# Two-layer transformer with experts: one gather of every four moved behind the scores, scalings spread over four waves, and a branch inside layer 1's run of waves

## The chip, the core and the metric

The kernel runs on one NeuronCore of one Trainium2 chip. The metric is the device time in microseconds of one execution. Three timed runs of the kernel before gave 1534.94, 1539.51 and 1540.47 us; the median is 1539.51 us. A separate execution was profiled.

## What is computed

Input is `x`, 8 sequences of 512 tokens with 256 features. Two layers follow each other, each an attention and a mixture of experts, each followed by a layer norm of (input + result). Cut to what matters here:

```python
x = layernorm(x + attn0(x))      # 16 heads of 16, causal towards later tokens (j >= i), softmax
x = layernorm(x + moe0(x))       # 7 experts 256->1024->256 with at most 512 tokens each, and a no-op expert; top 2
x = layernorm(x + attn1(x))      # rms norm, rotary, sigmoid scores divided by their sum
x = layernorm(x + moe1(x))       # 8 experts 256->512->256 and 4 that pass the token on; top 2
```

In `moe0` an expert takes the first 512 tokens, in order of the sequences, that chose it. If the first five sequences already fill every expert, the other three need not be dispatched. The kernel computes a flag `late` for the opposite case.

## The kernel before

**Waves.** Layer 0's attention runs as 8 x 16 waves (`waves0`, L1362). Wave `g` belongs to sequence `b = g // 16`, place `w = g % 16` in it. Four waves in a row are one group of four heads: `w // 8` is the half `m` of the features, `w // 4 % 2` the parity `t`. Within the group the four waves take the key blocks `jb` = 3, 2, 1, 0, with widths of 512, 384, 256 and 128 queries.

In each wave TensorE's order is written by hand (`tc.manual_schedule`), and each engine runs its own instructions in the order of the code:

1. `scores` (L583 on): four matmuls of the wave's width into two two-bank PSUM tiles `sc` (L588), an exponential for each on ScalarE (L597), a causal mask for each on GpSimd (L600, `affine_select`).
2. `lowered`, in waves with `w % 4 == 2`: four transposes (L580) into the bank `mm`, added to the queries by VectorE (L581).
3. the first steps of the plan.
4. `greatest` for the wave six ahead: four matmuls (L561) into two `sc` tiles, four reductions on VectorE (L569). Widths in the four waves of a group: 128, 256, 384, 512.
5. `gathered` for the wave before (kept in `waiting`): the exponentials times the values (L612), accumulated over the group in the bank `av`, widths 128, 512, 384, 256 in the four waves; after the last block ScalarE copies it out (L620).
6. the second steps of the plan.

PSUM has three `sc` tiles of two banks, one `av` and one `mm` bank in layer 0. The three `sc` tiles are taken in turn by scores and maxima, so that each use waits for the reader of the use three before. Every projection or transpose outside of 1, 4 and 5 goes through the one `mm` bank: the next such step waits until ScalarE or VectorE has emptied it.

**The plan.** `beside0` (L1290 on) lists for each place `w` the steps for other sequences: for the next one (`n`) its transposes (`turned_in`), queries and keys (`query`, one part of 256 tokens: 4 matmuls at L538, two evacuations on ScalarE at L545) and values (`value`, L521, copies at L525 and L530); for the last one (`a`) the way from attention to routing (`by_token`, `by_feature`, `projected`, `rooted`, `normed`, `logits`, `chosen`, `raised`); for the one before that (`z`) the rest of the routing and, from `w = 8`, the scatter of its rows to `xbuf` (L832, GpSimd's indirect DMA). `kept(b, c)` (L708) is the scaling of 128 tokens of the layer norm, in place, on ScalarE: 128x256 elements, four for each sequence.

**After seven sequences** come the seven experts of layer 0 (`experts0`), with a list of steps for sequences 5 and 6, one of which is taken at each of 50 gaps; then the eighth sequence's waves, with layer 1's first sequence prepared beside them; then layer 1's waves (`waves1`), in which `sc`, `av` and `mm` have two tiles each, and the gather of a wave stands behind the scores of the next.

**The branch.** After layer 1's first sequence, all engines load `late` into a register (L1656) and branch (L1657): if it is set, `again0` dispatches the last three sequences and runs the experts of layer 0 again. In this case's data it isn't set, and no instruction of `again0` appears in the trace. Ahead of it the last wave's gather is issued and the PSUM pools are closed; they are opened again behind it.

Of the kernel before, what the change touches and what calls it, by code (L numbers as in the profile page):

```python
# [43 lines left out]
def tile_two_layers(  # L44
# [41 lines left out]
    def psum(stack, sc, av, mm):  # L86

        for name, bufs in (("sc", sc), ("av", av), ("mm", mm)):
            p[name] = stack.enter_context(
                tc.tile_pool(name=f"p_{name}{sc}", bufs=bufs, space=PSUM)  # L90
            )
# [4 lines left out]
    def bank():  # L96
        return p["mm"].tile([P, 512], FP, tag="mm", name="mm")
# [1192 lines left out]
    def beside0(b, w):  # L1290

        z, a, n = b - 2, b - 1, b + 1
        t = l0
        plan = {
            -6: ([(t.value, n, 3)], []),
            -5: ([(t.value, n, 2)], []),
            -4: ([(t.value, n, 1)], [(t.query, n, 1, "q", 0)]),
            -3: ([(t.value, n, 0)], [(t.query, n, 1, "q", 1)]),  # L1300
            -2: ([], [(t.query, n, 1, "k", 0)]),
            -1: ([], [(t.query, n, 1, "k", 1)]),
            0: ([], [(t.turned_in, n, 0), (t.kept, z, 2), (t.kept, z, 3), (t.shared, z)]),
            1: ([(t.by_token, a, 0)], [(t.turned_in, n, 1), (t.pointed, z)]),
            2: ([], [(t.query, n, 0, "q", 0), (t.residual, n)]),
            3: ([(t.query, n, 0, "q", 1)], [(t.query, n, 0, "k", 0)]),
            4: ([(t.by_token, a, 1)], [(t.by_token, a, 2), (t.counted, z)]),
            5: ([(t.by_token, a, 3)], [(t.ranked, z)]),
            6: ([], [(t.query, n, 0, "k", 1), (t.sent, z)]),
            7: ([(t.by_feature, a, 0)], [(t.by_feature, a, 1)]),  # L1310
            8: ([(t.projected, a, 0)], [(t.projected, a, 1)]),
            9: ([(t.projected, a, 2)], [(t.projected, a, 3)]),
            10: ([], [(t.query, n, 1, "q", 0)]),
            11: ([(t.query, n, 1, "q", 1)], [(t.query, n, 1, "k", 0)]),
            12: ([(t.value, n, 3)], [(t.rooted, a)]),
            13: ([(t.value, n, 2)], [(t.normed, a), (t.logits, a)]),
            14: ([], [(t.query, n, 1, "k", 1), (t.chosen, a)]),
            15: (
                [(t.value, n, 1)],
                [(t.value, n, 0), (t.raised, a), (t.kept, a, 0), (t.kept, a, 1)],  # L1320
            ),
        }
        if b == B - 2:


            for i, lists in plan.items():
                plan[i] = tuple([s for s in steps if s[0] is not t.query] for steps in lists)
            plan[8] = ([(t.projected, a, 0)], [(t.query, n, 0, which, 0) for which in "qk"])
            plan[9] = ([(t.projected, a, 1)], [(t.query, n, 0, which, 1) for which in "qk"])
            plan[10] = ([], [(t.projected, a, 2)])  # L1330
            plan[11] = ([(t.projected, a, 3)], [])
        elif b == B - 1:

            u = l1
            plan = {
                0: ([], []),
                1: ([], []),
                2: ([], [(u.gather, 0, 0)]),
                3: ([], [(u.gather, 0, 1)]),
                4: ([], [(u.gather, 0, 2), (u.summed, 0, 0)]),  # L1340
                5: ([], [(u.gather, 0, 3), (u.summed, 0, 1)]),
                6: ([], [(u.summed, 0, 2)]),
                7: ([], [(u.summed, 0, 3)]),
                8: ([], [(u.normed, 0), (u.gather, 1, 0)]),
                9: ([], [(u.turned_in, 0, 0), (u.residual, 0), (u.gather, 1, 1)]),
                10: ([], [(u.turned_in, 0, 1), (u.gather, 1, 2)]),
                11: ([], [(u.query, 0, 0, "q", 0), (u.gather, 1, 3)]),
                12: ([], [(u.query, 0, 0, "q", 1)]),
                13: ([], [(u.query, 0, 0, "k", 0)]),
                14: ([], [(u.query, 0, 0, "k", 1)]),  # L1350
                15: ([], [(u.value, 0, 0), (u.value, 0, 1)]),
            }
        first, second = plan[w]
        if w >= 8 and z < EARLY:
            cs = [w - 8] if b < B - 2 else [2 * (w - 8), 2 * (w - 8) + 1]
            first = [(t.scatter, z, (c // 2, c % 2)) for c in cs if c < 2 * NC] + first
        return [[s for s in steps if 0 <= s[1] < B] for steps in (first, second)]
# [4 lines left out]
    def waves0(start, stop):  # L1362
        nonlocal waiting
        t = l0
        for g in range(start, stop):
            b, w = g // 16, g % 16
            now = None
            if g >= 0:
                now = t.scores(b, w // 8, w // 4 % 2, NC - 1 - w % 4)
                if w % 4 == 0:  # L1370
                    t.fill(b, w // 4)
                if w == 10 and b + 2 < B:
                    t.load_x(b + 2)
            if (g + 2) % 4 == 0 and 0 <= g + 2 < 16 * B:
                ob, ow = (g + 2) // 16, (g + 2) % 16
                t.lowered(ob, ow // 8, ow // 4 % 2)
            first, second = beside0(b, w if g >= 0 else g)
            if b == 0 and w in (1, 3, 4, 5, 8, 9, 12):
                fn, arg = t.rsteps.pop(0)
                fn(arg)  # L1380
                if w == 1:
                    t.residual(0)
            if b == 2 and w < len(l1.steps):
                fn, arg = l1.steps[w]
                fn(arg)
            run(first)
            ob, ow = (g + AHEAD) // 16, (g + AHEAD) % 16
            if ob < B:
                t.greatest(ob, ow // 8, ow // 4 % 2, (1, 0, 3, 2)[ow % 4])
            if waiting:  # L1390
                t.gathered(*waiting)
            run(second)
            waiting = now
# [76 lines left out]
                xes[e + 2] = tokens0(e + 2)  # L1470
        run(steps)

    def again0():


        with ExitStack() as ph:
            psum(ph, 1, 2, 2)
            rp = ph.enter_context(tc.tile_pool(name="redo", bufs=1))
            for b in range(EARLY, B):
                for c in range(NC):  # L1480
# [2 lines left out]
            for e in range(E0):  # L1483
# [6 lines left out]
                nc.sync.dma_start(out=xe, in_=xbuf[rows, :].rearrange("(c p) d -> p c d", p=P))  # L1490
                xeT = rp.tile([P, KC, S], FP, tag="xeT", name="xeT")
                for kc in range(KC):
                    ps = bank()
                    for c in range(NC):
                        nc.tensor.transpose(
                            ps[:, c * P : (c + 1) * P], xe[:, c, kc * P : (kc + 1) * P], ident
                        )
                    nc.vector.tensor_copy(xeT[:, kc, :], ps)
                for c in range(NC):
                    h = rp.tile([P, I0 // P, P], FP, tag="h", name="h")  # L1500
                    ps = wide().rearrange("p u (f t) -> p (u f) t", t=P)
                    for f in range(I0 // P):
                        for kc in range(KC):
                            nc.tensor.matmul(
                                out=ps[:, f, :], lhsT=wi[:, kc, f * P : (f + 1) * P],
                                rhs=xeT[:, kc, c * P : (c + 1) * P],
                                start=(kc == 0), stop=(kc == KC - 1),
                            )
                    nc.vector.tensor_scalar(h, ps, 0.0, None, ALU.max)
                    ps = bank()[:, :D]  # L1510
                    for f in range(I0 // P):
                        nc.tensor.matmul(
                            out=ps, lhsT=h[:, f, :], rhs=wo[:, f, :],
                            start=(f == 0), stop=(f == I0 // P - 1),
                        )
                    nc.vector.tensor_copy(xe[:, c, :], ps)
# [84 lines left out]
    with tc.manual_schedule():  # L1601
# [23 lines left out]
        steps = [(t.by_token, a, 0), (t.query, n, 1, "q", 0), (t.by_token, a, 1), (t.query, n, 1, "q", 1)]  # L1625
        steps += [(t.by_token, a, 2), (t.query, n, 1, "k", 0), (t.by_token, a, 3), (t.query, n, 1, "k", 1)]
        steps += [(t.by_feature, a, kc) for kc in range(KC)]
        steps += [(t.kept, z, c) for c in (2, 3)]
        steps += [(t.projected, a, c) for c in range(NC)]
        steps += [(fn, z) for fn in (t.shared, t.pointed, t.counted)]  # L1630
        steps += [(t.filled,)]
# [9 lines left out]
    rows1 = ExitStack()  # L1641
    l1p = rows1.enter_context(tc.tile_pool(name="l1p", bufs=1, side="right"))
    over = planp.tile([P, 1], I32, name="over")
    with tc.manual_schedule():
        waves0(16 * (B - 1), 16 * B)
        l0.gathered(*waiting)
        waiting = None
    banks.close()
    psum(banks, 2, 2, 2)
    with tc.manual_schedule():  # L1650
        waves1(0)
        l1.gathered(*waiting)
        waiting = None
    banks.close()
    alone.close()
    again = nc.values_load(late[0:1, 0:1], min_val=0, max_val=1)  # L1656
    with tc.If(again > 0):  # L1657
        again0()
    banks = ExitStack()
    psum(banks, 2, 2, 2)  # L1660
    ahead = ExitStack()
    lotp = ahead.enter_context(tc.tile_pool(name="lotp", bufs=1))

# [410 lines left out]
```

## Time and profile before

| What | Value |
|---|---|
| timed runs, median | 1539.51 us (1534.94 to 1540.47) |
| profiled execution | 1549.87 us |
| its span, first to last instruction | 1548.0 us |
| mean granted TensorE clock in it | 0.968 |
| first scores of sequences 1, 3, 4, 5 to those of the next (timeline) | 68.1, 70.1, 71.0, 71.7 us |
| layer 0's waves, sequences 0 to 6 / experts, first matmul to last / eighth sequence's waves | to 534 us / to 745 us / to 813 us |
| the branch on TensorE | 883 to 887 us |
| VectorE busy per 50 us in layer 0 (350 to 400 us) | 34.71 us |
| ScalarE, GpSimd, same stretch | 26.15, 18.89 us |

How to read it: a busy time is that of one engine, in the profiled execution. A group line gives the source line, the engine, the operation, what it writes and reads, how often, its busy time, the mean of one in ns, and the engine's idle time just before, with what ended most of it. A timeline line gives the start and the length in us, engine, line, operation, and in brackets the idle time before it and the engine, tile and line that ended that. PE is TensorE's matmuls, PEld its weight loads, PEq its instruction queue; ACT is ScalarE, DVE VectorE, POOL GpSimd. A line of windows gives a stretch, its length, the busy time of PE, PEld, DVE, ACT and POOL with their counts, the granted clock, the DMA share and GB/s. Four fp32 matmuls appear as eight instructions.

### The profile page before, as it was taken

What the parts mean: (1) busy time and instruction counts of PE and PEld (TensorE: products, weight loads), DVE (VectorE), ACT (ScalarE), POOL (GpSimd) and SP (SyncE); (2) the same over time, 40 slices, a digit from 0 to 9 for tenths busy, and PEclk for the clock granted to TensorE, in tenths of its full rate; (3) what the DMA queues carried; (4) which work ended last, traced back from release to release, by engine and by line L of the source; (5) the groups of instructions that cost most, each with busy time, mean ns of one, the idle gap of its engine ahead of it and who ended that gap; (6) DMA issues with size and microseconds to landing.
All of it is one profiled execution on the core that took longest, in us unless ns stands there. A gap on an engine that the chain in (4) does not pass through costs nothing. (4 is left out here: it accounts for less than half of the span.)

```text
span 1548.0 us, 24814 instructions
## 1 busy us (share of the span) xinstructions
PE 1414.4 (91%) x8574; PEld 759.5 (49%) x8574; DVE 877.7 (57%) x3287; ACT 689.6 (45%) x1079; POOL 480.7 (31%) x602
## 2 busy tenths in 40 slices
PE   7999889989998899999889899999999999999992
PEld 4444444444443466766434333333333344878881
DVE  4656666666766513121456466776766755553494
ACT  4455545454554321111335555666665666122242
POOL 2321233323233200000351224543643431342462
PEclk9999999999999999999989989999999999999996
DMA  8859950000000022231100000202302005557764
GB/s 245 250 164 361 356 187 13 19 7 25 2 22 4 29 82 82 82 120 57 42 28 8 22 8 30 38 27 23 46 22 28 19 16 158 182 179 241 271 221 158
DMA packets 136010, 149.86 MB, mean 97 GB/s; under 512 B 29645, under 2 KB 118890, under 8 KB 135874
## 3 DMA queue, kind: packets, MB, share of 16 engines
q1 hardware_dynamic: 118274, 121.51, 24.9%
q0 software_dynamic: 10560, 23.51, 6.2%
q10 hardware_dynamic: 7040, 3.15, 0.8%
q8 instruction: 72, 1.18, 0.3%
q14 instruction: 64, 0.52, 0.1%
HBM read 76.88 MB, written 77.10 MB: 99 GB/s over the span
## 5 line engine op out<-in xcount | busy, mean ns | idle before, releaser
L569 DVE CUSTOM_DVE_ANT_0 seen<-sc,shade 128x128 f32<-128x128 f32 (+3 forms) x512 | 251.1, 490 | 138.5 <-PE sc L561 109.8
L1035 ACT ACTIVATE e<-sc 128x1024 f32<-128x1024 f32 x256 | 248.5, 1021 | 150.3 <-PE sc L1027 139.9
L600 POOL TENSOR_SCALAR_AFFINE_SELECT e<-e 128x256 f32<-128x256 f32 x256 | 104.9, 416 | 590.0 <-ACT e L597 585.6
L597 ACT ACTIVATE e<-sc 128x1024 f32<-128x1024 f32 (+3 forms) x256 | 167.0, 702 | 125.9 <-PE sc L588 117.2
L1044 PE MATMUL av<-e,v 128*32 128x512 f32 x1024 | 140.7, 621 | 0.0
L561 PE MATMUL sc<-k,q 32*128 32x384 f32 (+3 forms) x1024 | 127.2, 499 | 12.7 <-DVE mpad L569 6.5
L588 PE MATMUL sc<-q,k 32*128 32x512 f32 (+3 forms) x1024 | 122.0, 491 | 3.6 <-DVE mpad L569 2.5
L612 PE MATMUL av<-e,v 128*32 128x512 f32 (+3 forms) x1024 | 99.4, 456 | 2.7 <-POOL e L600 2.3
L1753 PE MATMUL yp<-w_e,h 128*128 128x256 f32 x416 | 96.2, 384 | 3.0 <-DVE h L1745 3.0
L1457 PE MATMUL sc<-wo,h 128*128 128x256 f32 x448 | 98.7, 379 | 0.0
L1440 PE MATMUL sc<-xeT,wi 128*128 128x512 f32 x224 | 97.9, 592 | 0.0
L1737 PE MATMUL sc<-xtT,w_e 128*128 128x256 f32 x416 | 94.8, 380 | 0.2
L1457 PEld LDWEIGHTS sc<-wo,h 128*128 128x128 f32 x448 | 84.7, 190 | 11.7 <-issue 0.5
L1027 PE MATMUL sc<-q,k 16*128 16x512 f32 x512 | 82.6, 660 | 5.7 <-PEq L1657 2.2
L1027 PE MATMUL sc<-q,kb 32*128 32x512 f32 x512 | 81.4, 641 | 6.5 <-ACT e L1035 6.5
L1753 PEld LDWEIGHTS yp<-w_e,h 128*128 128x128 f32 x416 | 79.7, 193 | 14.9 <-DVE h L1745 3.8
L1764 POOL DMA_INDIRECT ybuf<-yt,to x52 | 51.0, 981 | 113.6 <-DVE yt L1763 101.8
L1737 PEld LDWEIGHTS sc<-xtT,w_e 128*128 128x128 f32 x416 | 77.1, 190 | 10.6 <-issue 1.2
L561 PEld LDWEIGHTS sc<-k,q 32*128 32x128 f32 x1024 | 52.7, 189 | 56.3 <-issue 25.4
L588 PEld LDWEIGHTS sc<-q,k 32*128 32x128 f32 x1024 | 49.3, 186 | 54.5 <-issue 33.6
L1210 POOL DMA_INDIRECT xbuf<-x,idx x64 | 68.4, 1068 | 23.7 <-issue 15.0
L898 POOL DMA_INDIRECT got<-ybuf,idx_all x64 | 65.7, 1027 | 17.3 <-issue 14.4
(304 smaller groups left out, 2094.5 us busy)
## 6 DMA issues: line engine op xcount, KB each, us to landing
xbuf<-blank SPq DMA_DIRECT2D x130, 272.0 KB
w_e<-in_w SPq DMA_DIRECT2D x104, 256.0 KB
ybuf<-blank SPq DMA_DIRECT2D x16, 512.0 KB
y<-ybuf SPq DMA_DIRECT2D x16, 512.0 KB
wi<-in_we_in SPq DMA_DIRECT2D x7, 1024.0 KB
wo<-in_we_out SPq DMA_DIRECT2D x7, 1024.0 KB
xt<-xbuf SPq DMA_DIRECT2D x26, 272.0 KB
own<-in_x SPq DMA_DIRECT2D x8, 512.0 KB
```

Source lines behind the costliest of these rows:

```text
L561: nc.tensor.matmul(out=places[r], lhsT=q["q", m, t][32 * r : 32 * r + 32, ib * P : (ib + 1) * P], rhs=q["k", m, t][32 * r : 32 * r + 32, i ...
L569: nc.vector.tensor_tensor_reduce(out=seen[:, :width], in0=places[r], in1=shade[:, :width], scale=-1.0, scalar=-MASKED, op0=ALU.add, op1=AL ...
L588: nc.tensor.matmul(out=places[r], lhsT=q["k", m, t][32 * r : 32 * r + 32, jb * P : (jb + 1) * P], rhs=q["q", m, t][32 * r : 32 * r + 32, : ...
L597: nc.scalar.activation(e[:, :, :width], s[:, :, :width], AF.Exp, scale=SCALE)
L600: nc.gpsimd.affine_select(out=own, in_=own, pattern=[[0, 2], [-1, P]], compare_op=ALU.is_ge, fill=0.0, base=0, channel_multiplier=1,)
L612: nc.tensor.matmul(out=q["av"][32 * r : 32 * r + 32, : (jb + 1) * P], lhsT=vs[b % 2][:, jb, 8 * m + 2 * r + t, :], rhs=es[r], start=(jb == ...
L1027: nc.tensor.matmul(out=scs[r // 2][:, r % 2, :], lhsT=k[32 * r : 32 * r + lanes, jb * P : (jb + 1) * P], rhs=q["q", m][32 * r : 32 * r + l ...
L1035: nc.scalar.activation(e, scs[pr], AF.Sigmoid, scale=SCALE)
L1044: nc.tensor.matmul(out=q["av"][32 * r : 32 * r + 32, :], lhsT=vs[b % 2][:, jb, 8 * m + 2 * r + t, :], rhs=es[r // 2][:, r % 2, :], start=( ...
L1457: nc.tensor.matmul(out=ps[:, c, :], lhsT=h[f][:, c * P : (c + 1) * P], rhs=wo[:, f, :], start=(f == 0), stop=(f == I0 // P - 1),)
L1737: nc.tensor.matmul(out=ps[:, f // 2, f % 2 * TB : (f % 2 + 1) * TB], lhsT=q.wi[kc][:, f * P : (f + 1) * P], rhs=q.xtT[:, kc, :], start=(kc ...
L1753: nc.tensor.matmul(out=q.ps[c], lhsT=q.h[:, f // 2, at : at + P], rhs=q.wo[f // 2][:, f % 2 * D : (f % 2 + 1) * D], start=(f == 0), stop=( ...
```

## The change

It has three parts. Nothing that is computed changes.

1. In `waves0`, in waves with `g % 4 == 3`, the gather of the wave before stands right behind the scores, ahead of the first steps and `greatest`. In the other waves it stays behind `greatest`.
2. In the plan, the four scalings `kept` of a sequence leave wave 15 (two of them) and wave 0 of the next sequence (two) for waves 2, 3, 6 and 7, one in each; they are last of their wave's second steps. One query part (key, part 1, `m` = 1) moves from wave 14 to wave 13, ahead of `normed` and `logits`. In the experts' step list, sequence 5 gets four scalings instead of two, since its wave 15 has none any more.
3. At the branch, the register load of `late` moves ahead of the eighth sequence's waves. The last gather of layer 1's first sequence isn't issued ahead of the branch but stays in `waiting`, so that it comes behind the first scores of the next sequence. The PSUM pools stay open; one `sc` and one `mm` tile are taken ahead of the branch for `again0`, which uses these two for everything.

The diff, cut to its core:

```diff
-            0: ([], [(t.turned_in, n, 0), (t.kept, z, 2), (t.kept, z, 3), (t.shared, z)]),
+            0: ([], [(t.turned_in, n, 0), (t.shared, z)]),
...
-            2: ([], [(t.query, n, 0, "q", 0), (t.residual, n)]),
-            3: ([(t.query, n, 0, "q", 1)], [(t.query, n, 0, "k", 0)]),
+            2: ([], [(t.query, n, 0, "q", 0), (t.residual, n), (t.kept, z, 0)]),
+            3: ([(t.query, n, 0, "q", 1)], [(t.query, n, 0, "k", 0), (t.kept, z, 1)]),
...
-            6: ([], [(t.query, n, 0, "k", 1), (t.sent, z)]),
-            7: ([(t.by_feature, a, 0)], [(t.by_feature, a, 1)]),
+            6: ([], [(t.query, n, 0, "k", 1), (t.sent, z), (t.kept, z, 2)]),
+            7: ([(t.by_feature, a, 0)], [(t.by_feature, a, 1), (t.kept, z, 3)]),
...
-            13: ([(t.value, n, 2)], [(t.normed, a), (t.logits, a)]),
-            14: ([], [(t.query, n, 1, "k", 1), (t.chosen, a)]),
-            15: (
-                [(t.value, n, 1)],
-                [(t.value, n, 0), (t.raised, a), (t.kept, a, 0), (t.kept, a, 1)],
-            ),
+            13: ([(t.value, n, 2)], [(t.query, n, 1, "k", 1), (t.normed, a), (t.logits, a)]),
+            14: ([], [(t.chosen, a)]),
+            15: ([(t.value, n, 1)], [(t.value, n, 0), (t.raised, a)]),
...
+            if g % 4 == 3 and waiting:
+                t.gathered(*waiting)
+                waiting = None
             if (g + 2) % 4 == 0 and 0 <= g + 2 < 16 * B:
...
-        steps += [(t.kept, z, c) for c in (2, 3)]
+        steps += [(t.kept, z, c) for c in range(NC)]
...
+    again = nc.values_load(late[0:1, 0:1], min_val=0, max_val=1)
     with tc.manual_schedule():
         waves0(16 * (B - 1), 16 * B)
...
     with tc.manual_schedule():
         waves1(0)
-        l1.gathered(*waiting)
-        waiting = None
-    banks.close()
     alone.close()
-    again = nc.values_load(late[0:1, 0:1], min_val=0, max_val=1)
+    places = wide(), bank()
     with tc.If(again > 0):
-        again0()
-    banks = ExitStack()
-    psum(banks, 2, 2, 2)
+        again0(*places)
```

Inside `again0`, `bank()` becomes the one `mm` tile and `wide()` the one `sc` tile, and its own pools go.

More of the change, by code (lines that the diff above doesn't have):

```diff
@@ L1471, in experts0, with again0 @@
         run(steps)
-    def again0():
+    def again0(inner, turned):
         with ExitStack() as ph:
-            psum(ph, 1, 2, 2)
             rp = ph.enter_context(tc.tile_pool(name="redo", bufs=1))
@@ L1492, in again0 @@
                 for kc in range(KC):
-                    ps = bank()
+                    ps = turned
                     for c in range(NC):
@@ L1500, in again0 @@
                     h = rp.tile([P, I0 // P, P], FP, tag="h", name="h")
-                    ps = wide().rearrange("p u (f t) -> p (u f) t", t=P)
+                    ps = inner.rearrange("p u (f t) -> p (u f) t", t=P)
                     for f in range(I0 // P):
@@ L1509, in again0 @@
                     nc.vector.tensor_scalar(h, ps, 0.0, None, ALU.max)
-                    ps = bank()[:, :D]
+                    ps = turned[:, :D]
                     for f in range(I0 // P):
```

## The prediction

> **What bounds the kernel now.** I read the page's busy table and slices first, then the groups of instructions by line, then the timeline over one sequence of layer 0 and over the branch. All sums below are made inside the profiled execution (span 1548.0 us, 1549.87 us with what lies around it). The median of the three timed runs is 1539.51 us, 0.7% less; I carry differences over to it unscaled.
>
> ```profile
> PE 1414.4 (91%) x8574; PEld 759.5 (49%) x8574; DVE 877.7 (57%) x3287; ACT 689.6 (45%) x1079; POOL 480.7 (31%) x602
> L561 PE MATMUL sc<-k,q 32*128 32x384 f32 (+3 forms) x1024 | 127.2, 499 | 12.7 <-DVE mpad L569 6.5 <-ACT e L597 5.5 <-ACT ye L1464 0.4
> L708 ACT ACTIVATE own<-own,less,r 128x256 f32<-128x256 f32 x32 | 17.5, 596 | 0.0
> ```
>
> TensorE is the bound, but not everywhere full. In layer 0 (to 534 us) it is some 90% busy. Adding up the bracketed idle times of the timeline by wave, sequences 3 to 5 lose 5.9 to 6.2 us each, of 70 to 72 us: 0.68 in each of waves 3, 7, 11 and 15, 0.91 in wave 14, 0.98 in wave 0, 0.29 in wave 1, 0.64 in wave 6, 0.33 in wave 9. In the expert stage it is 99% busy (49.65 of 50 us from 550 to 600), so nothing is won there.
>
> In a wave, S is the scores (L588), G the maxima's scores (L561, read by VectorE on L569), AV the gathered values (L612); the number is the width. The wave changed is S128, first steps, G512, AV256, second steps. Sequence 4, waves 3 and 4:
>
> ```profile
> 329.58 0.50 PE L588 MATMUL sc<-q,k 32*128 32x128 f32 x8
> 330.76 1.13 PE L538 MATMUL mm<-xT,wq_s 128*128 128x256 f32 x4 [0.68 <-ACT q L545]
> 331.82 1.14 PE L561 MATMUL sc<-k,q 32*128 32x512 f32 x8
> 332.90 0.64 PE L612 MATMUL av<-e,v 128*32 128x256 f32 x8
> 333.46 1.13 PE L538 MATMUL mm<-xT,wk_s 128*128 128x256 f32 x4
> 334.53 1.14 PE L588 MATMUL sc<-q,k 32*128 32x512 f32 x8
> 336.29 1.03 PE L561 MATMUL sc<-k,q 32*128 32x128 f32 x8
> ```
>
> There is one `mm` bank, and the first step waits 0.68 us for ScalarE to empty it of the last wave's query. AV256, 0.56 us of ready work, stands two places behind. The next excerpt is where wave 15 of one sequence meets wave 0 of the next:
>
> ```profile
> 316.47 1.08 ACT L708 ACTIVATE own<-own,less,r 128x256 f32<-128x256 f32 x2
> 317.42 0.49 PE L561 MATMUL sc<-k,q 32*128 32x128 f32 x4 [0.37 <-DVE mpad L569]
> 317.45 1.93 ACT L597 ACTIVATE e<-sc 128x1024 f32<-128x1024 f32 x2
> 318.52 0.49 PE L561 MATMUL sc<-k,q 32*128 32x128 f32 x4 [0.61 <-ACT e L597]
> 320.47 1.09 ACT L708 ACTIVATE own<-own,less,r 128x256 f32<-128x256 f32 x2
> ```
>
> The first tile of G128 waits for VectorE to read the last of G512; the second for the exponential of S512, which stands behind two scalings. Two more scalings stand ahead of the next exponential.
>
> At the branch (L1657):
>
> ```profile
> L1657 PEldq COMPARE_BRANCH  x1: 3717/3717/3717, 883.2 to 883.2; - x1
> 883.96 1.07 PE L1044 MATMUL av<-e,v 128*32 128x512 f32 x8
> 887.22 2.08 PE L1027 MATMUL sc<-q,k 16*128 16x512 f32 x6 [2.20 <-PEq L1657]
> 890.17 2.07 PE L1027 MATMUL sc<-q,k 16*128 16x512 f32 x2 [0.87 <-issue]
> 890.00:895.00 5.00, 4.83 (x10) 2.19 (x14) 0.00 (x0) 2.12 (x3) 0.00 (x0) 0.50 0.01 3
> ```
>
> TensorE's sequencer is held 3.7 us while the queue covers 1.8 of it; afterwards the clock stands at a half until about 901 us.
>
> **The change part by part.** *AV256 ahead of the first steps (waves 3, 7, 11, 15).* No work is added; 8 matmul instructions, 0.56 us, move into the 0.68 us hole. G512 does not start earlier for that: it stays behind the first step, which waits for the bank as before. What comes 0.56 us earlier is all after G512, and there the cover is gone. VectorE reads G512 with four reductions of 0.69 us plus a read of 0.08; they begin 1.18 after G512 starts, two are done at +2.6 and four at +4.2 (331.82, 333.00, 336.01). S512's second tile needs the two, G128's first tile the four, and G128's second the exponential of S512. So per place, with full-clock spacings from the timeline (S512 1.08, AV256 0.56, a projection 1.08, four transposes 0.6):
> - Wave 3 to 4: the second step starts at 333.05 (bank free), S512 at 334.13, by-token transposes done at 335.9, G128's first tile at 336.1 (VectorE). ScalarE: k evacuations to 335.2, then a scaling to 335.75, S512's exponential to 336.7; G128's second tile at 336.8, its end 0.15 us earlier than now. Gain 0.15 of 0.56.
> - Wave 7 to 8: the second step is only a transpose; S512's second tile already waits for VectorE (S512 starts at 280.04 and takes 1.56 instead of 1.14). Gain 0 to 0.1; I take 0.
> - Wave 11 to 12: two projections stand around it, S512's second tile comes just after the +2.6, G128 after the +4.2. Gain 0.4.
> - Wave 15: below.
>
> AV256 waits for GpSimd's mask of the wave before (done 291.9 in sequence 3, wave 10; needed 294.2), and has 2.3 us to spare.
>
> *Query k of part 1 from wave 14 to 13, scalings out of waves 15 and 0.* The projection (4 matmuls, 1.08 us; two evacuations, 1.02) leaves wave 14, where it waited 0.91 behind `lowered`, and wave 15's first step no longer waits 0.68. Against that: `lowered` in wave 14 now waits for the evacuations, 308.05 against TensorE's 307.5, so 0.55 of new idle; and S128's second tile needs two reductions of G384, which VectorE, busy with `normed` and `logits` until 309.1 in both orders, ends at 311.1. So S128 ends only 0.1 earlier, G512 starts at 312.95 for 313.18. From there: second step 314.02, S512 315.1 to 316.2 (now 317.0). On ScalarE value copies and `raised` end at 316.0, no scaling follows, S512's exponential ends at 317.3 (now 318.4); G128's first tile at 317.15 (VectorE), its end at 317.65 instead of 318.9. Then AV128, transposes, S384 at 318.66 for 319.88; its exponential no longer has 1.09 us of scalings ahead; wave 2 begins 7.45 us after S512's start. Now that distance is 8.6 (mean of the timeline's starts, sequences 1 to 5). Together 0.8 + 1.15 = 1.95 us for each such passage.
>
> *Scalings into waves 2, 3, 6, 7* (one each, 0.55 to 0.6 us on ScalarE, same number, no DMA). What they delay is the exponential behind them. In waves 3 and 7 the exponential of S128 gates G512's second tile: 331.65 against a need of 332.4, margin 0.75; in wave 7 margin 0.2. In waves 4 and 8 it is S512's exponential: wave 4 is counted above, in wave 8 a projection covers it. The scatters of own rows (L832), from wave 8, stay behind the last scaling in wave 7. If the cover were gone, each costs its 0.6.
>
> *Experts.* Two scalings more in the step list, 38 for 50 gaps; no step is left over. ScalarE is 16% busy there (8.02 of 50 us), each can delay a relu by up to 0.6; bounds 0 and 1.2 us; I take 0, as four such scalings for the same sequence and the next already lie there with TensorE at 99%.
>
> *Branch.* The load of `late` (490 ns on TensorE's queue) moves to where 7 us of expert matmuls are queued: 0, and at most 0.5. At the branch that load and the last AV512 (1.07 us) no longer stand ahead: the sequencer comes to it 0.75 earlier (about 882.45) and leaves at about 886.2, scores at 886.45 instead of 887.22; but the queue runs dry at 883.96 instead of 885.03, and AV512 still has to be done: 887.5 equivalent, so 0.3 us later. [...]
> The two PSUM tiles held for the branch's body have no row. They are free when the other engines have passed the branch (VectorE at 886.3, `sent` being queued before it), TensorE needs them at 886.45. Bounds: 0, and one slot's turn, an exponential of 1.0 us. I take 0.2. Branch in all 0.5 us slower, ends -7 and +2.5.
>
> **Sum.** Passages with scalings, 1 to 2 up to 5 to 6: 5 x 1.95 = 9.8. Passage 0 to 1 without: 0.8. Wave 3: 7 x 0.15 = 1.0. Wave 11: 6 x 0.4 = 2.4. Layer 0 gains 14.0; less 0.5 is 13.5. 1539.5 - 13.5 = 1526.
>
> **The rivals.**
> 1. *VectorE takes it all back.* G128 waits for G512's reductions wherever TensorE comes earlier; only the exponential's delay goes, 0.9 per passage: 5 x 0.9 = 4.5 us, 1535. For it: 0.37 `DVE mpad` at wave 0 already. Against: VectorE idles 1.85 us ahead of G512's reductions in wave 15.
> 2. *All of it stays.* 4 x 0.56 plus the 0.98, 0.29 and 0.91 less 0.55: 3.9 us in each of 6 sequences, 23 us, and a clock dip or two less (3.6 us at half clock at 320 and 453 us, after such idles): 1514. Against: the +4.2 of VectorE.
> 3. *Slower: the scalings land on the path.* In waves 2, 3, 6 and 7 each delays an exponential that TensorE waits for, while those removed were hidden behind VectorE anyway: 4 x 0.6 x 6 = 14.4 us, 1554. It decides once the margins of 0.75 (wave 3) and 0.2 us (wave 7) are used up, as by a query evacuation that comes late. For it: the 0.61 at wave 0 shows that an exponential behind scalings does stop TensorE. Against: the same row says that those removed were not hidden.
> 4. *Nothing:* gains are lost again at the next bound in the group; 1539.
>
> **How the numbers follow.** The forecast 0.52 (its own range 1520 to 1532), rival 1 0.20, rival 2 0.12, rival 3 0.11, rival 4 0.05. About 0.5% (7.7 us) is what a measurement of this kernel can tell from no change. Faster by that: the forecast but for its upper end, rival 2 and the better third of rival 1, 0.66; within: 0.23; slower 0.11. The range 1514 to 1541 leaves out half of rival 2 and all of rival 3; the branch's -7 lies in it.
>
> **What would show it.** Right: no 0.68 before the first steps of waves 3, 7, 11 and 15 (about 0.1 left); in wave 0 no wait for `ACT e`, but one of about 0.9 us for `DVE mpad`, since the cover moved; a new 0.55 for `ACT k` at L580 in wave 14; sequences 2 to 5 shorter by 2.5 us; the branch's idle at about 2.5 us. Wrong: new waits for `ACT e` at L561 in waves 3, 4, 7 or 8 (rival 3), waits for `DVE mpad` over 1.5 us in wave 0 (rival 1), or a half-clock stretch longer than 14 us after the branch.

## The result, and the profile after

The changed kernel took 1512.34 us (median of four runs, 1510.96 to 1514.48), the kernel before 1537.22 beside it (four runs, 1534.78 to 1540.47): 0.9838 of it, 95% interval 0.9811 to 0.9866, 24.9 us less. Two later comparisons on other chips gave 0.9874 [0.9835, 0.9913] and 0.9847 [0.9824, 0.9869]. The intervals overlap; some 23 us, nearly twice the forecast 13.5. The sign was right, the time lies just below the range.

The lines of the page (first two) and of the groups by line that answer to those shown before:

```profile
PE 1407.2 (93%) x8574; PEld 762.1 (51%) x8574; DVE 879.6 (58%) x3287; ACT 691.2 (46%) x1079; POOL 480.3 (32%) x602
L588 PE MATMUL sc<-q,k 32*128 32x512 f32 (+3 forms) x1024 | 140.6, 500 | 7.6 <-DVE mpad L569 7.0
...
L561 PE MATMUL sc<-k,q 32*128 32x384 f32 (+3 forms) x1024 | 120.8, 489 | 5.8 <-DVE mpad L569 4.6 <-ACT e L597 0.4 <-ACT ye L1464 0.4
L708 ACT ACTIVATE own<-own,less,r 128x256 f32<-128x256 f32 x32 | 18.6, 597 | 0.0
```

The line of the scores in the kernel before:

```profile
L588 PE MATMUL sc<-q,k 32*128 32x512 f32 (+3 forms) x1024 | 122.0, 491 | 3.6 <-DVE mpad L569 2.5 <-ACT e L597 0.4
```

The counts are the same: nothing was taken away. The maxima's scores (L561) waited 12.7 us before and 5.8 now; of that, the 5.5 us for the exponential are 0.4, and the 6.5 for VectorE are 4.6. But the scores (L588) now wait 7.0 us for `DVE mpad` where it was 2.5, and their busy time rose from 122.0 to 140.6 us with no more work. In wave 4 of sequence 4 the second tile's matmuls start at 398.18 us, 0.42 us behind the first tile's (0.01 in the kernel before); those of the first tile run until 398.89, and the engine counts as busy from 397.76 on. So part of the idle time moved to where a list of idle times doesn't show it. The timeline does. Waves 3 and 4 of sequence 4:

```profile
393.28 0.50 PE L588 MATMUL sc<-q,k 32*128 32x128 f32 x8
393.71 0.64 PE L612 MATMUL av<-e,v 128*32 128x256 f32 x8
394.46 1.13 PE L538 MATMUL mm<-xT,wq_s 128*128 128x256 f32 x4
395.52 1.14 PE L561 MATMUL sc<-k,q 32*128 32x512 f32 x8
396.70 1.13 PE L538 MATMUL mm<-xT,wk_s 128*128 128x256 f32 x4
397.76 1.55 PE L588 MATMUL sc<-q,k 32*128 32x512 f32 x8
```

The gather fills the 0.68 us hole. S512 starts 4.48 us after S128 (4.95 before), but takes 1.55 us instead of 1.14: its second tile waits for VectorE, whose second read of G512 ends at 398.12. And the passage from wave 15 to wave 0 (sequence 3 to 4):

```profile
309.41 0.64 PE L612 MATMUL av<-e,v 128*32 128x256 f32 x8
...
311.07 1.14 PE L561 MATMUL sc<-k,q 32*128 32x512 f32 x8
312.14 1.16 PE L521 MATMUL mm<-wv_s,xT 128*128 128x264 f32 x4
313.23 1.63 PE L588 MATMUL sc<-q,k 32*128 32x512 f32 x8
315.31 0.72 PE L561 MATMUL sc<-k,q 32*128 32x128 f32 x8 [0.45 <-DVE mpad L569]
```

The 0.61 for `ACT e` is gone, VectorE is what G128 waits for. At the branch, the sequencer's line and then the timeline and the windows behind it:

```profile
L1654 PEldq COMPARE_BRANCH  x1: 3357/3357/3357, 865.5 to 865.5; - x1
```

```profile
869.07 1.43 PE L1027 MATMUL sc<-q,k 16*128 16x512 f32 x8 [2.59 <-PEq L1654]
870.42 3.18 PE L1044 MATMUL av<-e,v 128*32 128x512 f32 x8
873.53 1.13 PE L999 MATMUL mm<-xnT,wq_s 128*128 128x256 f32 x4
```

```profile
870.00:875.00 5.00, 5.00 (x20) 1.31 (x20) 0.00 (x0) 2.83 (x4) 0.00 (x0) 0.66 0.01 3
875.00:880.00 5.00, 4.90 (x40) 1.88 (x36) 4.30 (x11) 3.26 (x5) 1.28 (x1) 1.00 0.00 0
```

There is one stop of 2.59 us and no second one, and the granted clock (third figure from the right: 0.66, then 1.00) is full again from 873.5 on, after 3.4 us; before, it stood at a half for 13.7 us (886.9 to 900.6).

To see the stages without what differs between chips, both kernels were run once more on one chip, with profiles (labels e13_before_again and e14_after_third). Their profiled runs took 1534.25 and 1509.77 us. A stage lasts from its first matmul to the first of the next:

| Stage (us, from the traces) | before | changed | difference |
|---|---|---|---|
| sequences 0 to 5 of layer 0 | 425.0 | 415.1 | -9.9 |
| sequence 6 | 71.8 | 71.2 | -0.6 |
| experts of layer 0 | 216.8 | 212.7 | -4.1 |
| eighth sequence | 66.4 | 67.1 | +0.7 |
| layer 1: first sequence | 69.9 | 69.2 | -0.7 |
| layer 1: second sequence (the branch) | 67.7 | 60.2 | -7.5 |
| layer 1: the rest | 579.1 | 576.9 | -2.2 |

Some 1.6 of the 4.1 is a half-clock stretch of 3.4 us at 678 us, which the first profile of the kernel before doesn't have (its expert stage takes 215.2 us). Layer 1's seventh sequence has one too (59.9 for 58.3), and so has the second sequence, at 923 us, behind the long one.

### The profile page after: what moved, and what is told of

Same layout as the page of the kernel before. It is cut to its first block, busy times and chain, and to the rows that moved or that the text cites. A ratio compares the mean times of both kernels' runs of the same rounds, so it can differ in the third digit from the quotient of the medians.

```text
span 1509.2 us, 24812 instructions
## 1 busy us (share of the span) xinstructions
PE 1407.2 (93%) x8574; PEld 762.1 (51%) x8574; DVE 879.6 (58%) x3287; ACT 691.2 (46%) x1079; POOL 480.3 (32%) x602
## 5 line engine op out<-in xcount | busy, mean ns | idle before, releaser
L600 POOL TENSOR_SCALAR_AFFINE_SELECT e<-e 128x256 f32<-128x256 f32 x256 | 104.8, 414 | 576.9 <-ACT e L597 574.0
L588 PE MATMUL sc<-q,k 32*128 32x512 f32 (+3 forms) x1024 | 140.6, 500 | 7.6 <-DVE mpad L569 7.0
L561 PE MATMUL sc<-k,q 32*128 32x384 f32 (+3 forms) x1024 | 120.8, 489 | 5.8 <-DVE mpad L569 4.6
L588 PEld LDWEIGHTS sc<-q,k 32*128 32x128 f32 x1024 | 57.9, 190 | 66.7 <-issue 36.7
L1748 PEld LDWEIGHTS yp<-w_e,h 128*128 128x128 f32 x416 | 79.8, 193 | 13.7 <-DVE h L1740 2.6
L1027 PE MATMUL sc<-q,k 16*128 16x512 f32 x512 | 77.4, 644 | 4.2 <-PEq L1654 2.6
L1027 PE MATMUL sc<-q,kb 32*128 32x512 f32 x512 | 77.3, 640 | 0.4 <-ACT e L1035 0.4
L561 PEld LDWEIGHTS sc<-k,q 32*128 32x128 f32 x1024 | 51.2, 186 | 47.0 <-issue 24.2
```

Source lines behind the costliest of these rows:

```text
L561: nc.tensor.matmul(out=places[r], lhsT=q["q", m, t][32 * r : 32 * r + 32, ib * P : (ib + 1) * P], rhs=q["k", m, t][32 * r : 32 * r + 32, i ...
L588: nc.tensor.matmul(out=places[r], lhsT=q["k", m, t][32 * r : 32 * r + 32, jb * P : (jb + 1) * P], rhs=q["q", m, t][32 * r : 32 * r + 32, : ...
L600: nc.gpsimd.affine_select(out=own, in_=own, pattern=[[0, 2], [-1, P]], compare_op=ALU.is_ge, fill=0.0, base=0, channel_multiplier=1,)
L1027: nc.tensor.matmul(out=scs[r // 2][:, r % 2, :], lhsT=k[32 * r : 32 * r + lanes, jb * P : (jb + 1) * P], rhs=q["q", m][32 * r : 32 * r + l ...
L1748: nc.tensor.matmul(out=q.ps[c], lhsT=q.h[:, f // 2, at : at + P], rhs=q.wo[f // 2][:, f % 2 * D : (f % 2 + 1) * D], start=(f == 0), stop=( ...
```

## The experiments

**Each part alone.** Edits: only the block `if g % 4 == 3 and waiting` (e1_av); only the plan and the experts' list (e2_plan); only the branch (e3_branch); the first two together (e4_layer0).

> Part 1 alone: the gather moved behind the scores in every fourth wave; plan and branch as before. My theory on record (most of a gather's 0.56 us comes back as a wait for VectorE's reductions of G512): 0.15 in wave 3, 0 in wave 7, 0.4 in wave 11, about 0.3 in wave 15 to 0, over 6 to 7 sequences 4 to 6 us less than before. Rival 'all of it stays': 4 x 0.56 in 6 sequences, 13 us less. Third theory, the branch gives what layer 0's sum lacks: 4 to 6 us as in the first.

> Part 2 alone: scalings in waves 2, 3, 6, 7 and the key query in wave 13; gather and branch as before. Theory on record: 5 passages from wave 15 to wave 1 at about 1.2 us (exponentials no longer behind scalings, waits of 0.91 and 0.68 gone, 0.55 new), so 6 us less; scalings in waves 3 and 7 cost nothing. Rival 'all of it stays': 8 to 10 us less. If scalings land on the path: 0 to 8 us more.

> Part 3 alone: the branch with PSUM pools open and the last gather behind the first scores; layer 0 as before. Theory on record: 0.5 us more, ends -7 and +2.5. Third theory: this part gives the 11 us by which the change beat the forecast, so 8 to 12 us less; the trace then shows either a shorter half-clock stretch after the branch (13.8 us before) or shorter waves in layer 1's later sequences.

> Parts 1 and 2 together, branch as before. Theory on record: 14 us less. Rival 'all of it stays': 23 us less and nothing from the branch. Third theory: about 14 less, the rest of the 25 us from the branch.

The last column is the ratio times the median of the kernel before on the same chip, 1544.92 us.

| | ratio to before, 95% | us |
|---|---|---|
| e1_av | 0.9962 [0.9944, 0.9980] | -5.9 |
| e2_plan | 0.9939 [0.9915, 0.9963] | -9.4 |
| e3_branch | 0.9971 [0.9955, 0.9988] | -4.5 |
| e4_layer0 | 0.9894 [0.9867, 0.9921] | -16.4 |

The three add up to 19.8 us. The gather is about what was expected. The plan is more than its 6 us by its middle, though its interval (5.7 to 13.1) takes them in; the branch, expected at 0.5 us more, is clearly faster. The trace of the plan shows two places: sequences 0 to 5 take 3.7 us less, the expert stage 211.8 us for 215.2.

**Plan taken apart.** The four scalings alone, with the experts' list (e5_kept), and the query alone:

```diff
-            13: ([(t.value, n, 2)], [(t.normed, a), (t.logits, a)]),
-            14: ([], [(t.query, n, 1, "k", 1), (t.chosen, a)]),
+            13: ([(t.value, n, 2)], [(t.query, n, 1, "k", 1), (t.normed, a), (t.logits, a)]),
+            14: ([], [(t.chosen, a)]),
```

> Of part 2 the scalings alone (waves 2, 3, 6, 7 instead of 15 and 0); the query stays in wave 14. Theory on record: the exponential of S512 in wave 0 and of S384 in wave 1 come 1.1 us earlier, 0.9 us gained in each of 5 passages, none lost in waves 3 and 7: 4.5 us less. If the scalings land on the path in waves 3 and 7: no change or up to 5 more. If the passage gives its full 1.95 already by this: 9 less.

> Of part 2 the query alone (wave 13 instead of 14); scalings stay in 15 and 0. Theory on record: 0.91 and 0.68 of idle go, 0.55 and a wait of S128 for VectorE come, so 0.1 to 0.2 us earlier at wave 15 in 6 sequences: 1 us less. If the query gives what the scalings don't: 4 to 5 less.

Scalings 0.9941 [0.9919, 0.9962], 9.1 us less; query 0.9962 [0.9942, 0.9983], 5.9 less; together 9.4. That is less than the sum, but each of the three is uncertain by some 3 us, and in the traces the two add up: waves 13 to 1 of a full sequence take 22.68 us before, 21.83 with the scalings moved, 21.94 to 22.20 with the query moved, 21.09 to 21.34 with both (e2) and 21.26 with the whole change. The expert stage is 211.8 us with the scalings and 215.6 with the query, so its 3.4 us come with the two more scalings in the list.

**The expert stage: scalings or shift?** The kernel before with two empty steps in the experts' list:

```diff
+        steps += [(lambda *_: None, z) for _ in range(2)]
         steps += [(t.projected, a, c) for c in range(NC)]
```

> The kernel before, with two steps that do nothing put into the step list of the experts ahead of sequence 5's projections, where the change has two more scalings: nothing is computed differently, the later steps only come two gaps later. If the 3 us that the expert stage gained with the change come from this shift of the steps, the stage takes about 212 us here (215.2 before) and the whole 3 us less than the kernel before; if they come from the scalings themselves (that sequence 5's last two are done in the expert stage and not in its wave 15), the stage stays at 215 and the time is the kernel's before within 1 us.

The stage took 212.6 us, so the shift of the later steps by two gaps gives 2.6 of the 3.4 us. The group of the rank counts' matmul in the expert stage, kernel before (again), then with the empty steps:

```profile
L789 PE MATMUL mm<-took,before 128*128 128x32 f32 x4 | 0.8, 287 | 1.8 <-DVE took L779 1.4 <-DVE least L827 0.4
```

```profile
L789 PE MATMUL mm<-took,before 128*128 128x32 f32 x4 | 0.6, 234 | 0.0
```

`counted` stood one gap behind a VectorE step that wasn't done yet, and TensorE waited 1.8 us. That is 1.8 of the 2.6; the rest we could not place. The whole kernel was 0.9949 [0.9932, 0.9966], 7.3 us less by the medians, and more than the stage gives. Its profiled run (1532.1 us), taken on another chip, is only 2.1 us shorter than that of e13, and where its other stages differ, half-clock stretches lie in other places; where the other 4 to 5 us are stays open.

**The branch taken apart.** The kernel before with open pools and early load, but the gather ahead of the branch as before (e7); the changed kernel again on that chip (e8):

> Of part 3 the open PSUM pools alone: the last gather of layer 1's first sequence stays ahead of the branch, so that TensorE's queue is as long at the branch as before. [...]

> The changed kernel once more, beside the parts of it. If the three parts only add up (5.9 + 9.4 + 4.5 us by the runs so far), it is 20 us less than before. If there is a fourth term, the wait for the query's evacuation in wave 11 of layer 1's sequences, which the profile of the changed kernel alone does not show (0 against 0.1 to 1.1 us of TensorE idle, and 58.3 us a sequence against 59.6 to 62), it is 24 to 26 us less, and this profile again shows 58.3 us in sequences 2 to 5. If that wait is a matter of chance in each execution, it shows up here too in some sequences.

e7 0.9983 [0.9964, 1.0002], unclear; e8 0.9874 [0.9835, 0.9913]. The time of e7 alone does not tell it from e3's 0.9971, as the intervals overlap. The traces do: with the open pools alone the clock stays at a half for 13.7 us again, and layer 1's second sequence takes 66.9 us, for 66.3 in the first profile of the kernel before and 63.6 in e3. So the open pools alone are not what counts. Next, the changed kernel with the kept gather first behind the branch (e9), and with the routing one wave earlier (e10):

```diff
+            if b == 1 and w == 0:
+                l1.gathered(*waiting)
+                waiting = None
             now = l1.scores(b, w // 8, w // 4 % 2, w % 4)
```

```diff
-                13: ([], [], [(u.pointed, a)]),
-                14: ([], [], [(u.counted, a)]),
-                15: ([], [], [(u.ranked, a), (u.sent, a)]),
+                13: ([], [], [(u.pointed, a), (u.counted, a)]),
+                14: ([], [], [(u.ranked, a), (u.sent, a)]),
```

> The changed kernel, but behind the branch the kept gather (four matmuls of 128 rows and 512 columns, 1.07 us) is issued ahead of the first scores (of 16 rows) and not behind them. Theory (gathers of 128 rows early behind the branch are what brings the clock back): the half-clock stretch is at most 7 us, perhaps 3.4, and the time is 0 to 3 us less than the changed kernel's. Rival (what counts is only that TensorE reaches the branch earlier, or chance): the stretch lies anywhere from 3.4 to 17 us, without regard to the order. If the scores must come first to give ScalarE work, 0.5 to 1 us more than the changed kernel's.

> The changed kernel, but in layer 1's first sequence the last steps of the routing ahead of the branch come one wave earlier (counted in wave 13, ranked and sent in wave 14), so that TensorE's sequencer meets the branch with more matmuls still queued. Theory: the idle time of TensorE at the branch falls from 2.6 to about 1 us, and the half-clock stretch behind it shrinks or goes: 1.5 us less than the changed kernel's by the idle time alone, up to 5 less with the clock. [...]

e9: 0.9867 [0.9852, 0.9882], but it does not do what was meant. In its instruction stream the gather came out ahead of the branch:

```profile
865.35 1.06 PE L1044 MATMUL av<-e,v 128*32 128x512 f32 x8
868.26 1.55 PE L1027 MATMUL sc<-q,k 16*128 16x512 f32 x7 [1.85 <-PEq L1657]
871.19 1.22 PE L1027 MATMUL sc<-q,k 16*128 16x512 f32 x1 [1.37 <-issue]
```

It became the changed kernel with only the gather's place undone: the second stop is back (1.37 <-issue), and the half-clock stretch is 10.2 us instead of 3.4 to 6.8. Its second sequence of layer 1 takes 62.8 us, for 60.2, 61.8 and 62.4 in the three profiles of the changed kernel. e10: 0.9821 [0.9807, 0.9835], 1507.74 us, idle 0.99, no half-clock stretch, second sequence 58.9 us, as its theory had it.

The same edit on the kernel before (e16), and on the changed kernel with the scaling of wave 3 moved to wave 5 (e15), beside both kernels unchanged:

> The kernel before, unchanged, with a profile from the same chip as the next three. Theory: the stall in wave 11 of layer 1's first six sequences (1.3 us each, about 8 us in all) belongs to the chip, not to the kernel, so the kernel before shows it here exactly when the changed kernel does; without it layer 1 from the branch to the end takes some 8 us less than in the first profile. Rival: only the kernel before has it, and its absence is part of the change's gain.

> The changed kernel, unchanged, a third time, on the same chip as the kernel before. Theory: 19 to 25 us less than it; the difference without the stall is one of half-clock stretches, and a comparison of the two profiles of one chip by stages gives 9 to 9.5 us in the first six sequences, 3 in the expert stage, 3 to 7 at the branch. If the difference is 25 and these three stages give only 19, the rest lies elsewhere and is to be named.

> The changed kernel with the routing one wave earlier ahead of the branch, and the scaling of wave 3 in wave 5. Theory: the branch's idle is 1 us without a half-clock stretch, as in the run with the earlier routing alone (about 4 us less than the changed kernel), and waves 3 and 4 take 8.16 us and not 8.44 (as in the run with the gather alone), 0.28 x 6 = 1.7 us less, unless the scaling delays wave 5's exponential by the same: then 0. Together 4 to 6 us less than the changed kernel.

> The kernel before with the routing one wave earlier ahead of the branch, nothing else. Theory (what counts at the branch is how much is queued while the branch holds TensorE's sequencer): the idle falls from 2.2 to 1 us or less and the half-clock stretch of 13.8 us goes or shrinks to 3.6: 3 to 8 us less than the kernel before, with PSUM pools closed and the register loaded as before. Rival (the open pools and the gather behind the scores are needed for it): idle stays above 2 us, the stretch above 10, and the time is the kernel's before within 1.5 us.

e13 0.9998 [0.9979, 1.0017]; e14 0.9847 [0.9824, 0.9869]; e15 0.9846 [0.9821, 0.9871], 1509.64 us; e16 0.9944 [0.9926, 0.9962], 8.6 us less than the kernel before by this two-wave edit alone. In e16 the idle is 2.01 and not 1, yet the clock doesn't fall (1.00 in each window of 5 us from 880 to 895 us):

```profile
882.50 1.05 PE L1044 MATMUL av<-e,v 128*32 128x512 f32 x2
885.56 1.06 PE L1044 MATMUL av<-e,v 128*32 128x512 f32 x6 [2.01 <-PEq L1656]
886.55 1.13 PE L999 MATMUL mm<-xnT,wq_s 128*128 128x256 f32 x4
```

All eighteen profiles at the branch:

| | idle of TensorE (us) | half-clock stretch (us) |
|---|---|---|
| gather ahead of the branch: before twice, e1, e2, e4, e5, e6, e7, e9, e11 | 1.85 to 2.32, then 0.8 to 2.1 more inside the first scores | 10.2 to 17.1 |
| gather behind the first scores: changed three times, e3, e12 | one stop, 2.57 to 2.99 | 3.4 to 6.8 |
| routing one wave earlier: e10, e15, e16 | 1.0, 1.0, 2.0 | none |

Where the stretches begin helps to read this table. Within one profile all of them begin on one grid with steps of 3.41 us, and all but the one at the kernel's end are whole steps long: in the first profile of the kernel before those at 183.8, 197.4, 320.3 and 453.4 us lie 4, 40 and 79 steps behind the first. Where the grid lies differs from one execution to the next. Here is the step ahead of the fall in the first profiles of the kernel before and of the changed one, and then the two steps of e16 on which its stop lies:

```profile
883.48:886.90 3.42, 1.54 (x13) 0.57 (x11) 1.20 (x8) 0.59 (x1) 0.00 (x0) 1.00 0.02 5
866.65:870.06 3.41, 0.99 (x8) 0.48 (x8) 1.06 (x8) 0.00 (x0) 0.00 (x0) 1.00 0.03 7
881.14:884.55 3.41, 2.41 (x10) 0.81 (x6) 1.39 (x6) 1.94 (x2) 0.00 (x0) 1.00 0.03 7
884.55:887.97 3.42, 2.41 (x14) 1.02 (x18) 0.00 (x0) 0.00 (x0) 0.00 (x0) 1.00 0.02 5
```

In the fifteen profiles with a stretch behind the branch TensorE was busy for 0.4 to 1.6 us of the step ahead of it. In e16 the stop falls across a border of the grid and leaves 2.4 us on either side; inside one step it would have left 1.4, by the same count. So that e16 kept its clock may be luck, and no run shows what the same stop does elsewhere on the grid. A stop of 1.0 us, as in e10 and e15, takes at most that from a step, and 2.4 us were left. Busy time alone is no rule, though: in the first profile of the changed kernel the clock fell at 900.8 us after a step with 2.9 us busy. And the edit also changed what runs right behind the stop: three quarters of the gather in e16, half a projection in e10 and e15, all with 128 rows, where the other fifteen have the scores with 16.

In e15 waves 3 and 4 take 8.16 us for 8.43, as expected, but waves 5 and 6 take 9.11 for 8.81, and sequences 3 to 5 take 68.15 for 68.13. The 0.3 is the same in e1, where no scaling stands in wave 5: another wait there takes back what wave 3 gains, so the scaling in wave 3 costs nothing in the end. Together e15 was level with the changed kernel on the same chip, and its profiled run 2.3 us shorter; so e10's edit is not shown to be faster than the changed kernel itself on one chip. It has a shorter second sequence (58.8 to 58.9 us for 60.2 to 62.4), and beside e12 below, the changed kernel with another edit, it took 4.2 us less on one chip (1506.5 to 1509.5 for 1511.4 to 1513.7).

**A stall that belongs to the chip.** In the first profile of the kernel before, in wave 11 of layer 1's fourth sequence, ScalarE's query evacuation starts 2.43 us late:

```profile
1053.46 1.94 ACT L1035 ACTIVATE e<-sc 128x1024 f32<-128x1024 f32 x2 [2.17 <-PE sc L1027]
1057.83 0.69 ACT L1006 ACTIVATE raw<-mm,bq_s 128x512 f32<-128x512 f32 x1 [2.43 <-PE sc L1027]
```

Its projection (L999) had ended at 1055.1; TensorE's semaphore updates of that time all appear at 1057.7 to 1057.9, after GpSimd's last of eight indirect gathers. It costs about 1.3 us in each of six sequences (59.7 for 58.3). Two explanations were tried: the gathers in close succession (spread over waves 6, 8, 10 and 12), and the chip.

> The changed kernel, but GpSimd's gathers of layer 1's rows, eight in waves 6 to 9 of each of its sequences, stand in waves 6, 8, 10 and 12, two in each. If the stall of 1.1 to 2.7 us on ScalarE in wave 11 (a finished query projection is told late) comes from the eight gathers in close succession, it is gone or lies elsewhere in smaller pieces: 6 to 8 us less than the changed kernel on the same chip, when that shows the stall; nothing less when it doesn't. Rival: the telling is late for another reason and the stall stays in wave 11; time within 1 us of the changed kernel's. If the stall moves behind the last gather (wave 12 or 13) at full size, it follows the end of the gathers, not their packing.

e12: 0.9850 [0.9836, 0.9863], 1511.92 us, no stall; but e9 to e11, with packed gathers on the same chip, had none either, nor had e13 and e14. The stall is in the first profile of the kernel before and in all of e1 to e8, on other chips, in both kernels; the kernel before has a median of 1545 us on the chips of e1 to e8, and of 1536 to 1537 on those of e9 to e16, which fits 6 x 1.3 us. So the spreading is untested, the stall is no part of the change, and why some chips show it is open.

## Why the prediction was right in sign and short in size

The forecast was 13.5 us less, the result 24.9. The steps that failed are the two terms put at about nothing: the experts (0, measured 2.6 less) and the branch (0.5 more, measured 4.5 less alone and 7.5 less in the pair of profiles). The large term, layer 0's waves, had its mechanism right and was put too high (14.0, measured 9.5). That these errors have opposite signs is luck, and so is some of the rest: 3.2 us of the pair's difference are half-clock stretches that only the kernel before happened to have.

Measured from e13 to e14 (one chip) and from sequences at full clock:

| Step of the sum | predicted | measured |
|---|---|---|
| wave 3 to 4, each | -0.15 | -0.18 in sequences 2 to 5, -0.45 in 0 and 1; sum -1.6 for 1.0 |
| wave 7 to 8 | 0 | 0.00 |
| wave 11 to 12, each | -0.4 | -0.33, in five; sum -1.65 for 2.4 |
| passage with scalings, each | -1.95 | -1.42 in four; -0.6 in the one from 1 to 2 |
| passage 0 to 1 | -0.8 | 0.0 |
| experts | 0 (0 to +1.2) | -2.6 |
| branch | +0.5 (-7 to +2.5) | -4.5 [-7.0, -1.9] alone; -7.5 in the pair of profiles |

**The waves: mechanism right, two terms mis-sized.** VectorE's readings at +2.6 and +4.2 did limit the gain as the prediction said: no 0.68 but 0.11 before the first steps, `ACT e` gone in wave 0, the new wait for `ACT k` in wave 14 (0.47 for 0.55), and `DVE mpad` in wave 0 at 0.45, half of the 0.9 (the other half is inside S512's 1.63 us). Rival 1 (VectorE takes it all back) and rival 3 (the scalings land on the path) fell, by these rows and by e15. Rival 2's 1514 is nearest to the measured time, but not for its reason: of its 3.9 us in a sequence 1.9 stayed (70.04 to 68.13 in sequence 3 at full clock). The passage was mis-sized in two places. G512 was to start 0.23 us earlier: it starts 11.33 us after wave 13 in both traces, so from there to wave 0 only the gather's 0.56 is won, not 0.8. And wave 2 begins 7.77 us after S512, not 7.45. The prediction took five equal passages; sequence 2 has VectorE steps of its own (waits for `turns`, 0.8 us in wave 1), so the passage from 1 to 2 gives a third. The passage from 0 to 1 gives none: its 0.8 was carried over from the others without a look at its own waves. By these terms layer 0's waves gave 9.5 us (1.6 + 1.65 + 4 x 1.41 + 0.6) in place of 14.0. In the pair of profiles it is 10.5, since the kernel before has two half-clock stretches at 323 and 456 us, 2.2 us together, that the changed one has not (rival 2 named them), and the changed one loses 1 to 2 elsewhere.

**The experts: the step that failed in sign.** "ScalarE is 16% busy there, each can delay a relu; bounds 0 and 1.2" looked only at the two added instructions. It missed that a list taken one step per gap is shifted by them, and that a step's distance to its producer is part of its cost. The profile showed the 1.7 us at L789 in the "99% busy" stage.

**The branch: right idle time, wrong clock.** The idle was forecast at 2.5 us and measured at 2.59, in part by luck: it goes with the time for which the branch holds the sequencer, 3.36 us there, and was 2.86 and 2.99 where that was 3.70 (e8, e12) and 3.84 (e3). Two things under it were wrong. The load of `late` didn't move: on TensorE's queue it is at 864.9 us, right ahead of the branch at 865.5, although its line stands ahead of the eighth sequence; its place in the source didn't set it here. And the 2.2 us row, to which 0.3 us was added, was taken as if it were the whole stop. The kernel before had a second stop of 0.87 us, in the excerpt shown, 2 us later, which goes with the gather's place (ten profiles with it, eight without). It is no cause of the fall, since the clock fell at 886.9 us and the second stop began at 889.3 (so in eight of the ten; in e1 and e2 the fall comes later). What changed is the way back: the stretch shrank from 13.7 us (17.1 in e13) to 3.4 (6.8 in e8). The sum put nothing down for the clock, and no run shows the term behind its lower end of -7; the runs showed 4.5 us less [1.9 to 7.0] with the branch alone and 7.5 in the pair of profiles. The length of one stop doesn't order the cases: 2.59 us of idle in the changed kernel cost 3.4 us of half clock, 2.01 in e16 none. Nor did busy time alone bring the clock back: in the first profile of the kernel before TensorE is busy through two whole steps of the grid, 890.31 to 897.14 us, and the clock stays at 0.50 for one more. The windows of the kernel before, again, behind its branch:

```profile
890.00:895.00 5.00, 5.00 (x16) 2.20 (x16) 1.65 (x3) 2.05 (x3) 1.27 (x1) 0.50 0.00 0
895.00:900.00 5.00, 5.00 (x23) 1.65 (x21) 2.95 (x10) 1.60 (x2) 0.00 (x0) 0.50 0.00 0
```

TensorE is busy 10 of 10 us here too, and the clock stays at 0.50. What brings it back stays open: the length of the stops, the rows in use behind them (16 in the scores, 128 in the gather) and the place on the grid are not separated. e9 was to do it and did not.

The pair's 24.5 us is then accounted for: 10.5 for the waves, 2.6 for the experts, 7.5 for the branch (with the stretch at 923 us), 3.2 for two stretches of the kernel before (at 678 us and in the seventh sequence of layer 1); the eighth sequence and layer 1's first cancel, and 0.7 remain. Half-clock stretches make up nearly half of it by estimate (most of the branch's 7.5, as 17.1 us at half clock became 3.4, and the 3.2), and they differ from one execution to the next. That may be why the parts alone, 19.8, and the whole, 19 to 26 by medians, agree only within their intervals.

## What to carry to other kernels

Adding a step to a list that is taken one per gap moves all behind it: check each moved step against its producer, since that can be worth more than the step (here 2.6 of 3.4 us). At a branch, look at the work queued in front of it on the engine whose sequencer it holds longest (here TensorE's, 3.36 to 3.96 us), and at what that engine does in the microseconds behind it: here the clock cost more than the idle (in the first profile of the kernel before 13.7 us at half clock, some 7 us by estimate, for 2.20 and 0.87 us of idle), and how much differed between executions of one kernel (13.7 and 17.1 us at half clock). When an engine's idle time falls, look whether the busy time of a neighbouring group grew (here from 122.0 to 140.6 us at L588), since a wait inside a group hides there; and compare profiles of one chip before putting microseconds down to a change.

## What the runs showed that was not expected

- The branch held TensorE's sequencer for 3.36 to 3.96 us in eighteen profiles, VectorE's for 0.07, ScalarE's for 0.06.
- Half-clock stretches came in steps: 3.4, 6.8, 10.2, 13.7 and 17.1 us behind the branch, and 20.5 in the eighth sequence of three profiles, all multiples of 3.41, on a grid that was fixed within an execution.
- Semaphore updates of TensorE arrived up to 2.6 us late, in a burst, in all profiles of two chips and in none of two others.
- The same kernel before measured 1536 to 1545 us by chip, 0.6%: more than several of the parts studied here.
